# A few loads moved to another queue, and transposes placed in two waits of TensorE, in a four-layer graph network

## The chip, the cores and the metric

The kernel runs on one core of one Trainium2 chip. The metric is the device time of one execution in microseconds (us). Executions of one kernel differ by some 0.1 to 0.2%, so each timed comparison interleaves runs of both kernels on the same chip.

## The reference, cut to what matters

128 graphs of 128 nodes with 256 features, fp32, share one adjacency matrix. Four layers follow each other; each normalises its input, applies one kind of graph network and adds the result to the input.

```python
# x: (128, 128, 256), adj: (128, 128)
h = relu(layernorm(x)); x = x + gated_gnn(h, adj, ...)        # layer 0
h = relu(layernorm(x)); x = x + attention(h, adj, ...)        # layer 1
h = relu(layernorm(x)); x = x + three_graph_convs(h, adj, ...)# layer 2
h = relu(layernorm(x))                                        # layer 3
t = einsum('nm,bmd->bnd', A_hat, h).reshape(-1, 256)
z = t @ W1.T + b1                                             # 16384 x 512
z = relu(batchnorm(z, g1, be1))      # statistics over all 16384 rows
o = z @ W2.T + b2
x = x + batchnorm(o, g2, be2)        # statistics over all rows again
```

The batch norms divide the program. No row of the first can be normalised before the last row of `z` is known. So `z` goes to device memory tile by tile in pass one and is loaded again in pass two, and `x` (called x3 below) waits in device memory for the last stage.

## The kernel before: the parts that matter

The kernel treats 32 groups of 4 graphs. Its instructions are interleaved by strings of letters: each letter takes the next step of one stream (a layer of a group, or the preparation of weights). The head, with the first groups in layers 0 and 1 and nothing else to do, is:

```python
FILL = "acpacaacacaccabpcpbdbddAddbAddbbbAdAbAbAdpAbpdpp"
for k in FILL:
    next(stream[k])
```

Pass one ends each group with four partial products per half (a Strassen-like scheme with seven products), sums them into one of two buffers `z[j]` and stores them from SyncE's queue. The store must have landed before the buffer is written again, by the next group's sum on VectorE (L725):

```python
z = ZT[g] = [zp.tile([P, 2, T], FP, tag="z", ...) for j in range(2)]   # pool zp: 2 buffers
def put(ij, pb, other):
    ...
    nc.vector.tensor_tensor(dst, pb, other, ALU.add)                   # L725
    ...
    if g != LAST:
        nc.sync.dma_start(Z[g][:, 2 * j : 2 * j + 2, :], z[j])         # L731
```

Between the passes:

```python
bw2T = second_w.tile([P, FC, D], FP, name="bw2T")
nc.sync.dma_start(bw2T, BW2T)              # weights of the second product, 512 KB
bw2s = second_w.tile([P, 3, FC // 2, D // 2], FP, name="bw2s_late")
nc.sync.dma_start(bw2s, BW2S)              # their sums, 384 KB
...
def load_x3(g, queue=nc.gpsimd):           # 512 KB of x for the last stage
    ...
    queue.dma_start(R[g], X3[g]...)
...
for n in range(1, 1 + AT_ONCE):
    load_z(n)                              # 1 MB of z, on SyncE's queue
sc1, sh1 = bn_affine(...)                  # scale and shift of the batch norm
... second(g): ScalarE relu(scale z + shift) (L859), three VectorE sums,
    seven products on TensorE (L870)
    ...
    if n % 4 == 3 and n // 4 < IN_PASS:
        load_x3(n // 4)                    # 8 of the x3 loads: GpSimd's queue
```

The instructions are written in this order, but a scheduler places those of each engine, so a load may be issued well before the place where it stands.

## Time and profile before

| | us |
|---|---|
| time, median of 3 runs (range) | 2611.72 (2609.52 to 2614.7) |
| profiled span | 2610.6 |
| TensorE busy | 2534.5 (97%) |
| TensorE's wait before the last product of pass one | 4.46 |
| TensorE's wait for the batch norm | 6.31 |
| half clock in the head | 25.2 to 38.8 and 55.9 to 69.5 |
| half clock between the passes | 2325.7 to 2339.4 |

The first three rows say that only 76 us of idle time are to be had. The two waits of TensorE are between the passes. (The last two rows come from the clock records. The prediction gives the ends of these stretches some 0.45 us too late: the windows that it shows agree with the records, 0.62 in 68:70 being half clock up to 69.5.) The lines of the profile stand in the prediction.

### The profile page before, as it was taken

The page shows a single profiled execution, that of the slowest core. Times are in us where ns is not written, and L with a number is a line of the kernel's source. Part 1 is how long each engine was busy: PE and PEld are TensorE (multiplying, and loading weights), DVE is VectorE, ACT ScalarE, POOL GpSimd, SP SyncE. Part 2 cuts the span into 40 slices and gives each one's busy share as a digit, 9 for nine tenths or more (in the row PEclk, how much of TensorE's full clock was granted, in tenths as well). Part 3 has the DMA queues.
Part 4 walks back from the last instruction along what each step waited for, and adds up shares of the span by engine and source line. Part 5 has one row for each costly group of instructions (what it writes and reads, how often), then busy time and mean ns, then how long its engine had stood idle before and what let it go on. Part 6 is the DMA issues. An engine that isn't in the chain of part 4 may idle for free. (4 is left out here: it accounts for less than half of the span.)

```text
span 2610.6 us, 40551 instructions
## 1 busy us (share of the span) xinstructions
PE 2534.5 (97%) x15209; PEld 2278.0 (87%) x15209; DVE 1914.1 (73%) x4820; ACT 1283.5 (49%) x2575; POOL 296.9 (11%) x589
## 2 busy tenths in 40 slices
PE   5999999999999999999999999999999999989996
PEld 3899999999999999999999999999999999868875
DVE  6777777777777777777777777777777776557776
ACT  4544554444445544454444444544445443336656
POOL 2110111111110111111111111111011111010001
PEclk8999999999999999999999999999999999989998
DMA  3000000000000000000000000010000000044459
GB/s 132 15 33 33 33 25 25 33 33 33 31 26 26 33 33 33 33 33 22 28 33 33 33 26 25 32 33 33 33 33 33 17 25 25 25 151 162 170 180 392
DMA packets 49560, 143.06 MB, mean 55 GB/s; under 512 B 4162, under 2 KB 23124, under 8 KB 45396
## 3 DMA queue, kind: packets, MB, share of 16 engines
q1 hardware_dynamic: 41012, 112.28, 11.8%
q0 software_dynamic: 7632, 27.79, 3.0%
q8 instruction: 120, 1.97, 0.3%
q14 instruction: 76, 0.62, 0.1%
q10 hardware_dynamic: 720, 0.39, 0.1%
HBM read 73.48 MB, written 66.98 MB: 54 GB/s over the span
## 5 line engine op out<-in xcount | busy, mean ns | idle before, releaser
L338 ACT ACTIVATE h<-x,sh,rs 128x256 f32<-128x256 f32 x512 | 268.9, 589 | 371.5 <-POOL sh L335 371.5
L397 PE MATMUL p_x<-uT,w 128*128 128x256 f32 x1024 | 242.2, 379 | 0.0
L672 ACT ACTIVATE h2T<-h2T 128x512 f32<-128x512 f32 x192 | 120.5, 628 | 228.9 <-DVE h2T L671 228.4
L397 PEld LDWEIGHTS p_x<-uT,w 128*128 128x128 f32 x1024 | 189.7, 190 | 23.2
L327 DVE BATCH_NORM_STATS2 st<-x 128x6 f32<-128x256 f32 x512 | 191.2, 415 | 4.3 <-DMA x<-in_x_dram 2.1
L331 POOL TENSOR_SCALAR rs<-mv 128x4 f32<-128x4 f32 (+1 forms) x131 | 31.5, 240 | 1396.3 <-ACT h2T L672 1026.8
L449 DVE SCALAR_TENSOR_TENSOR gs<-h,gw 128x256 f32<-128x256 f32 x384 | 161.2, 420 | 33.6 <-ACT h L338 27.6
L412 ACT COPY p_t<-p_x 128x512 f32<-128x512 f32 (+1 forms) x192 | 96.7, 504 | 108.4 <-PE p_x L397 101.6
L332 POOL TENSOR_TENSOR rs<-rs,nhalf 128x4 f32<-128x4 f32 (+1 forms) x131 | 149.8, 1144 | 0.0
L352 PEld LDWEIGHTS pmu<-a2T,u 128*128 128x128 f32 x1024 | 119.4, 192 | 15.3 <-issue 15.1
L380 PEld LDWEIGHTS p_x<-w,h2T 128*128 128x128 f32 x1024 | 124.3, 192 | 3.3
L859 ACT ACTIVATE zi<-zi,sh_bn,sc_bn 128x512 f32<-128x512 f32 x124 | 97.5, 813 | 55.5 <-DMA zi<-z 35.6
L380 PE MATMUL p_x<-w,h2T 128*128 128x128 f32 x1024 | 124.6, 275 | 0.0
L625 ACT ACTIVATE u<-u 128x512 f32<-128x512 f32 x93 | 58.7, 631 | 133.7 <-DVE u L624 133.7
L397 PE MATMUL p_x<-us,w_s 128*128 128x256 f32 x512 | 121.3, 379 | 0.0
L397 PE MATMUL p_z<-us,w 128*128 128x256 f32 x512 | 121.2, 379 | 0.0
L397 PE MATMUL p_x<-uT,w_s 128*128 128x256 f32 x512 | 121.1, 379 | 0.0
L397 PE MATMUL p_y<-uT,w 128*128 128x256 f32 x512 | 121.0, 379 | 0.0
L397 PE MATMUL p_z<-us,w_s 128*128 128x256 f32 x512 | 120.9, 379 | 0.0
L352 PE MATMUL pmu<-a2T,u 128*128 128x128 f32 x1024 | 119.5, 275 | 0.0
L701 DVE TENSOR_TENSOR x<-pr,x 128x512 f32<-128x512 f32 x64 | 43.7, 683 | 90.4 <-PE pr L700 90.4
L397 PEld LDWEIGHTS p_z<-us,w 128*128 128x128 f32 x512 | 97.2, 190 | 13.6 <-ACT p_t L412 0.4
(298 smaller groups left out, 6174.7 us busy)
## 6 DMA issues: line engine op xcount, KB each, us to landing
z<-zo SPq DMA_DIRECT2D x62, 512.0 KB, 2.6
zi<-z SPq DMA_DIRECT2D x31, 1024.0 KB, 5.0
x<-x POOLq DMA_DIRECT2D x32, 512.0 KB, 3.4
x<-in_x_dram SPq DMA_DIRECT2D x31, 512.0 KB, 4.0
out_dram<-x3i SPq DMA_DIRECT2D x30, 512.0 KB, 12.0
x3i<-x POOLq DMA_DIRECT2D x21, 512.0 KB, 8.4
x3i<-x SPq DMA_DIRECT2D x11, 512.0 KB, 4.5
w<-in_L_gnn_W_dram SPq DMA_DIRECT2D x1, 2048.0 KB
```

The source lines that it names most:

```text
L327: nc.vector.bn_stats(st[:, k, :], xt[:, b, :])
L332: nc.gpsimd.tensor_tensor(rs, rs, nhalf[:, :n], ALU.pow)
L338: nc.scalar.activation(h[:, b, :], xt[:, b, :], AF.Relu, bias=sh[:, k : k + 1], scale=rs[:, k : k + 1])
L352: nc.tensor.matmul(pm[:, k, :], src[:, b, c * P : (c + 1) * P], aT, start=True, stop=True)
L380: nc.tensor.matmul(pb[:, rr, :], a_r[r][:, c, rr * P : (rr + 1) * P], b_r[r][:, c, :wide], start=(first and rr == 0 and c == 0), stop=(c = ...
L397: nc.tensor.matmul(pb[:, jj, :], b_r[r][:, c, at : at + P], a_r[r][:, c, :], start=(first and jj == 0 and c == 0), stop=(c == nk - 1), ski ...
L412: nc.scalar.copy(t, pb)
L449: nc.vector.scalar_tensor_tensor(gs, h[:, b, :], 1.0, gw[:, i, :], ALU.mult, ALU.mult, accum_out=gl[:, k, i : i + 1],)
L625: nc.scalar.activation(dst, dst, AF.Relu)
L672: nc.scalar.activation(dst, dst, AF.Relu)
L701: nc.vector.tensor_tensor(xt[:, 2 * q : 2 * q + 2, :], pr, xt[:, 2 * q : 2 * q + 2, :], ALU.add)
L859: nc.scalar.activation(z, z, AF.Relu, bias=sh1[:, j : j + 1], scale=sc1[:, j : j + 1],)
```

## The change

It has three parts. Queues: the first `z` load goes ahead of the weights, and the x3 loads leave GpSimd's queue for SyncE's, behind the `z` loads. Sixty transposes of the identity, whose result nobody reads, keep TensorE busy in the wait at the batch norm. Twelve more fill a wait in the head.

```diff
+    def awake(n):
+        pw = bank([P, P], "awake")
+        for _ in range(n):
+            tc.keep_in_program_order(nc.tensor.transpose(pw, ident, ident))
...
-    FILL = "acpacaacacaccabpcpbdbddAddbAddbbbAdAbAbAdpAbpdpp"
+    FILL = "acpacaacacaccabpcpbdbddAddbAddbbbAdwAbAbAdpAbpdpp"
...
     for k in FILL:
-        next(stream[k])
+        if k == "w":
+            awake(12)
+        else:
+            next(stream[k])
...
     last1 = bn_part(stats1, FC, slice(LAST - 1, NG), "last1")
+    awake(60)
...
-    nc.sync.dma_start(bw2T, BW2T)
...
-    nc.sync.dma_start(bw2s, BW2S)
...
-    for n in range(1, 1 + AT_ONCE):
+    load_z(1)
+    nc.sync.dma_start(bw2T, BW2T)
+    nc.sync.dma_start(bw2s, BW2S)
+    for n in range(2, 1 + AT_ONCE):
         load_z(n)
...
-            load_x3(n // 4)
+            load_x3(n // 4, nc.sync)
```

## The prediction

> **What bounds the kernel now.** I read the page first: TensorE's share, the granted clock, what moves by slice.
>
> ```profile
> PE 2534.5 (97%) x15209; PEld 2278.0 (87%) x15209; DVE 1914.1 (73%) x4820; ACT 1283.5 (49%) x2575; POOL 296.9 (11%) x589
> PEclk8999999999999999999999999999999999989998
> GB/s 132 15 33 33 33 25 25 33 33 33 31 26 26 33 33 33 33 33 22 28 33 33 33 26 25 32 33 33 33 33 33 17 25 25 25 151 162 170 180 392
> ```
>
> TensorE is busy 97% of the span; it is the bound nearly everywhere. Its clock falls in the head (slice 1), between the passes (slice 36) and at the end, where 392 GB/s move and the DMA engines are the bound. A change off the matmuls can only win where TensorE stands idle (2610.6 - 2534.5, some 76 us in all) or runs slow. So I went to these places in the timeline. Between the passes (start us, us, engine line op out<-in):
>
> ```profile
> 2317.93 1.18 POOL L848 DMA_DIRECT2D x3i<-x  x2 [3.79 <-issue]
> ...
> 2319.44 0.38 SPq L826 DMA_DIRECT2D bw2T<-BW2T  x1
> ...
> 2326.82 0.69 DVE L725 TENSOR_TENSOR zo<-pz_z,pz_t 128x512 f32<-128x512 f32 x1 [4.06 <-DMA z<-zo]
> ...
> 2328.16 2.08 PE L397 MATMUL pz_x<-gT,bw1T_s 128*128 128x256 f32 x4 [4.46 <-DVE zo L725]
> ...
> 2335.68 2.93 ACT L859 ACTIVATE zo<-zo,sh_bn,sc_bn 128x512 f32<-128x512 f32 x4 [4.82 <-DVE sh_bn L806]
> ...
> 2336.55 2.08 PE L870 MATMUL po_x<-zo,bw2T 128*128 128x256 f32 x4 [6.31 <-ACT zo L859]
> ```
>
> TensorE idles twice: 4.46 us before the last product of pass one, 6.31 us for the batch norm. The first is a DMA wait at second hand: VectorE may not write the last z tile until the store of its buffer has landed. In a narrower window of the same view that store is issued at
>
> ```profile
> 2319.03 0.32 SPq L731 DMA_DIRECT2D z<-zo  x1
> ```
>
> and frees VectorE at 2326.8, 7.8 us later; the page's median for this store is 2.6 us. Two x3 loads of 512 KB are in flight beside it from GpSimd's queue (2317.93) and two weight loads (896 KB) follow it on SyncE's. The granted clock here, in windows of one us (PE, PEld, DVE, ACT, POOL busy, PEclk, DMA share, GB/s):
>
> ```profile
> 2325.00:2326.00 1.00, 0.00 (x0) 0.00 (x0) 0.00 (x0) 0.00 (x0) 0.00 (x0) 0.87 1.02 418
> 2339.00:2340.00 1.00, 1.00 (x6) 0.83 (x5) 0.97 (x3) 1.00 (x3) 0.00 (x0) 0.81 1.03 410
> ```
>
> The clock is 0.50 from 2326.2 to 2339.8, and 418 GB/s say that the DMA engines are full while VectorE waits. The head:
>
> ```profile
> 58.95 2.14 PE L352 MATMUL pm<-a2T,h 128*128 128x128 f32 x8
> 63.77 1.22 PE L352 MATMUL pm<-a2T,h 128*128 128x128 f32 x4 [2.67 <-ACT h L338]
> 65.84 0.85 PE L482 MATMUL pc<-ident,m 128*128 128x128 f32 x3
> 66.48 5.11 PE L635 MATMUL pu<-w,mT 128*128 128x512 f32 x8
> 71.43 1.89 PE L490 MATMUL pm<-h,m 128*128 128x256 f32 x8
> ...
> 75.40 2.06 ACT L639 ACTIVATE u<-pu 128x512 f32<-128x512 f32 x4 [8.94 <-DVE x L494]
> ...
> 80.16 1.04 PE L224 MATMUL bw1T<-ident,wide 128*128 128x128 f32 x8
> ```
>
> with the clock of these stretches:
>
> ```profile
> 56.00:58.00 2.00, 1.48 (x4) 1.01 (x5) 1.69 (x7) 0.47 (x2) 1.43 (x3) 0.50 0.00 0
> 68.00:70.00 2.00, 2.00 (x4) 0.86 (x3) 0.00 (x0) 0.00 (x0) 0.00 (x0) 0.62 0.00 0
> ```
>
> Half clock up to 69.98; from 63.8 on TensorE never stops again, so a microsecond won here stays won as long as TensorE is the bound. Last, the stage that consists of transposes alone:
>
> ```profile
> 2544.00:2545.50 1.50, 0.95 (x3) 0.56 (x4) 0.00 (x0) 1.50 (x3) 0.00 (x0) 0.50 1.01 410
> 2547.00:2548.50 1.50, 1.50 (x12) 1.50 (x11) 1.34 (x3) 1.50 (x3) 0.00 (x0) 0.80 1.01 412
> ```
>
> **What the Trainium skill says.** (1) "TensorE: Matmul & The Clock Gate", Part 1: an idle array falls to half clock, and a busy window of about 3.4 us, counted on a free-running grid, restores it. The trace agrees: half-clock stretches last 13.65 us (56.3 to 69.98, 2326.2 to 2339.8), four windows of 3.41. (2) Same page, Part 4, on the transpose: full clock does not engage for transpose mode, it "doesn't count as PE-busy the same way". The trace contradicts it: at 2544.5 transposes begin, nothing else runs on TensorE, and the clock is full from about 2548. I go by the trace; otherwise both added runs of transposes would be pure cost. (3) "DMA: Bandwidth & Descriptors", Queues, rings and completion order: each DMA engine takes turns between queues with work and serves one ring in order. The trace agrees: the store had one other store ahead of it on its own queue and still took 7.8 us beside GpSimd's loads; and of three 1 MB zi loads issued 0.42 us apart at 2328.2, the tile view of z gives 6.8 and 8.9 us to landing for two, so they land 2.5 us apart, in turn.
>
> **The change, part by part.**
> Queues. The order of instructions shows eight x3 loads moved from GpSimd's queue to SyncE's, six of them behind the third zi load; the first zi load now goes ahead of bw2T and bw2s. That zi load waits for the last VectorE sum of pass one, as before (2328.17 after a sum that ended at 2328.1), so everything behind it waits too, and the last z store has the engines to itself. It lands at about 2319.03 + 2.6 = 2321.6. VectorE's next limits are its own statistics, ended 2322.76 (2326.82 less the wait of 4.06), and TensorE's pz_z, ended 2322.83; so the sum starts at 2322.9 instead of 2326.8. The second sum needs pz_x, ended 2323.7, and ends at 2324.45 instead of 2328.1. The last pz_x then starts 3.7 us earlier and at full clock (idle 0.75 us): 1.03 us instead of 2.08. It ends at 2325.5 instead of 2330.24: 4.7 us. What follows up to ScalarE's first L859 took 2335.68 - 2330.24 = 5.44 us of ScalarE, VectorE and GpSimd, unchanged: L859 at 2330.95.
> Weights. The first zi load is issued at 2324.5 and lands 4.7 us on (the 5.0 of the page, 6.8 less 2.5 plus the 0.4 between issues): 2329.2. bw2T, half as large, 1.25 later: 2330.5; bw2s 2331.4. They are needed at about 2331.8 and 2334.6. Hidden, by 1.3 us.
> Sixty transposes. At full clock eight take 1.04 us, one alone 0.27, so 0.11 each; sixty are 6.6 us, from 2325.3 to 2331.9. ScalarE's first tile is ready at 2330.95 + 0.8 = 2331.75. They just fill the wait. What the warm clock buys is small: the first products wait for ScalarE's four L859 (2.93 us) and then for three VectorE sums of 0.69, cold or warm; by then the cold clock had recovered. Worth 0.1 us.
> Twelve transposes in the head. They start when the first pm ends, 60.9. At half clock one costs (0.85 - 0.42)/2 = 0.215, so 2.6 us, to 63.5: within the wait that ends at 63.77. TensorE is then busy from 58.95 without a break, and the grid point at 63.1 restores the clock instead of that at 69.98. The eight pu go from 66.48-71.43 (four of them at 0.86) to about 65.3-68.7: 2.7 us. The chain behind it (pm L490, VectorE L492, L494, then ScalarE's u, which waited 8.94 us for L494) moves with it. The grid's phase differs by run, so I take 2.2.
> The second pass is TensorE's (59.92 us busy in the 60 from 2340), the last stage the DMA engines'; both start earlier and cost the same. Sum: 4.7 + 0.1 + 2.2 = 7.0, from 2611.7 to 2604.7.
>
> **Rivals.**
> The fill overruns. If transposes do not hold the clock, sixty cost 12.9 us, the first po_x comes at 2338.2, some 6 us late: the gain between the passes is eaten, about 2610. Against it: the last stage's clock.
> The weights become the new wait, behind 1 MB of z. For it: a margin of 1.3 us, on estimates. Each microsecond late costs one: 2606 to 2608.
> The store is slow for its own reasons, not for the loads beside it. Then the sum still waits until 2326, only the head wins: 2609. Against it: the median of 2.6 us.
> The head's clock falls anyway or VectorE becomes its bound (9.8 of 10 us busy from 90 to 100): 2607.
>
> **Range.** The two gains are nearly independent; the middle is the surer. Three runs of before lie within 5 us. I take 2602.0 to 2609.0. The change has some 7 us to win and at worst a few to lose, against 52 us for 2%: 0.01, 0.98, 0.01.
>
> **What would show it.** Right: VectorE's L725 waits under 1 us for z<-zo; po_x begins near 2332 in the trace's time (less the head's gain, near 2330), right behind the sixty; clock 1.0 through the gap; in the head full clock by 66 and pm L490 near 69. Wrong: po_x waiting for a DMA, a fill at 0.2 us a transpose, an L725 that still waits 4 us, or pu still at 0.86 each.

## The result, and the profile after

| | before | changed |
|---|---|---|
| median of 4 runs each (range) | 2612.47 (2609.52 to 2614.7) | 2605.47 (2605.08 to 2607.53) |
| ratio, 95% interval | | 0.9975 [0.9958, 0.9993] |
| profiled span | 2610.6 | 2603.0 |

A ratio is the mean time of one kernel's runs over that of the other's in the same rounds, so not quite the ratio of the medians. By the threshold of 2% this is "the same"; in microseconds it is 7.0 by the medians. Measured again in a later series, the changed kernel took 2606.32 (6 runs) and the kernel before 2611.17 (10 runs), ratio 0.9982 [0.9969, 0.9994]. That is 4.9 us, so the gain is known to about 2 us from totals alone.

In the changed kernel the line numbers are higher by 7 up to the end of pass one (L725 became L732, L352 became L359) and by 9 in pass two (L859 is L868, L870 is L879); the transposes are L92. The page of the changed kernel, same three lines as in the prediction:

```profile
PE 2538.9 (98%) x15281; PEld 2283.6 (88%) x15281; DVE 1914.1 (74%) x4820; ACT 1283.8 (49%) x2575; POOL 291.3 (11%) x581
...
PEclk8999999999999999999999999999999999999998
...
GB/s 133 15 33 33 33 28 22 33 33 34 33 25 25 33 33 33 33 33 21 29 33 33 33 25 25 33 33 33 33 33 25 25 25 25 25 136 181 175 172 395
```

The 8 of slice 36 in the clock row has become a 9. TensorE has 72 instructions more and is 4.4 us longer busy in a span that is 7.6 us shorter: the work that was added stands where there was idle time. The timeline between the passes (start us, us, engine line op out<-in):

```profile
2313.74 2.12 SPq L738 DMA_DIRECT2D z<-zo  x2
...
2319.45 0.69 DVE L732 TENSOR_TENSOR zo<-pz_z,pz_t 128x512 f32<-128x512 f32 x1 [0.21 <-PE pz_z L404]
...
2321.00 1.13 PE L404 MATMUL pz_x<-gT,bw1T_s 128*128 128x256 f32 x4 [0.78 <-DVE zo L732]
2321.01 0.32 SPq L845 DMA_DIRECT2D zi<-z  x1
2321.42 0.38 SPq L902 DMA_DIRECT2D bw2T<-BW2T  x1
...
2321.97 6.71 PE L92 MATMUL awake<-ident 128*128 128x128 f32 x60
...
2327.55 2.93 ACT L868 ACTIVATE zo<-zo,sh_bn,sc_bn 128x512 f32<-128x512 f32 x4 [4.79 <-DVE sh_bn L817]
...
2328.52 1.30 PE L879 MATMUL po_x<-zo,bw2T 128*128 128x256 f32 x4
```

VectorE's sum L732 no longer waits for a store but, 0.21 us, for TensorE's own product. TensorE waits 0.78 us in place of 4.46, and runs its last product at 1.13 in place of 2.08 us. The sixty transposes take 6.71 us and end 0.16 us after po_x begins (ends of matmuls are modelled): they fill the wait and no more. Windows of the clock (us, PE, PEld, DVE, ACT, POOL busy, PEclk, DMA share, GB/s):

```profile
2320.00:2321.00 1.00, 0.22 (x2) 0.00 (x1) 0.85 (x3) 0.00 (x0) 0.00 (x0) 1.00 0.00 0
...
2324.00:2326.00 2.00, 2.00 (x20) 2.00 (x19) 1.37 (x10) 0.00 (x0) 0.34 (x1) 1.00 1.00 412
...
60.00:62.00 2.00, 1.62 (x15) 1.39 (x13) 2.00 (x9) 0.85 (x3) 1.49 (x4) 1.00 0.00 0
```

In the first, where the stall was, nothing moves on the DMA engines; in the second the clock is at 1.00 with transposes alone; the third is the head. The head's timeline:

```profile
58.35 1.96 PE L359 MATMUL pm<-a2T,h 128*128 128x128 f32 x8 [0.37 <-ACT h L345]
...
60.15 1.47 PE L92 MATMUL awake<-ident 128*128 128x128 f32 x12
...
62.87 0.71 PE L359 MATMUL pm<-a2T,h 128*128 128x128 f32 x4 [1.25 <-ACT h L345]
...
64.43 3.70 PE L642 MATMUL pu<-w,mT 128*128 128x512 f32 x8
...
67.97 1.89 PE L497 MATMUL pm<-h,m 128*128 128x256 f32 x8
...
71.94 2.06 ACT L646 ACTIVATE u<-pu 128x512 f32<-128x512 f32 x4 [7.39 <-DVE x L501]
```

The eight pu take 3.70 us in place of 5.11, and the second pm begins at 67.97 instead of 71.43. To see where the 7.5 us of the two profiled spans lie, I cut both at the same instructions: the first product of layer 0's last mixing (pm), the first product of layer 2 (pmu, which ends the head's low clock), GpSimd's last store of x3 in pass one, the first normalised tile (L859/L868), the first ScalarE instruction of the last stage.

| stretch | before | changed | gain |
|---|---|---|---|
| start to pm | 58.95 | 58.35 | 0.60 |
| pm to pmu (head) | 17.64 | 14.78 | 2.86 |
| pmu to last x3 store (2235 us of dense work) | 2234.67 | 2234.65 | 0.02 |
| last x3 store to first normalised tile | 24.42 | 19.77 | 4.65 |
| first normalised tile to the last stage | 208.01 | 208.27 | -0.26 |
| last stage | 66.88 | 67.21 | -0.33 |
| sum | 2610.57 | 2603.03 | 7.54 |

The 0.60 lies ahead of everything that was changed; the start of one execution differs from that of the next. What the head won is still won 2235 us later.

The -0.26 is smaller than the spread of its stretch. Four kernels run pass two with the same order of instructions on every engine and at full clock throughout (the changed kernel, its repeat below, and below those without the twelve and with a third fill), and they took 208.27, 208.27, 208.90 and 207.90 us in it. They drift apart only later in the pass: their first 28 matmuls (seven products of four each, the same in every kernel told of here) take the same time, and the 29th begins 9.02 to 9.03 us after the first normalised tile. In the kernel before it begins after 8.73. I therefore read pass two from this mark as well.

### The profile page after: what moved, and what is told of

Its sections match the earlier page's. It is cut to its first block, busy times and chain, and to the rows that moved or that the text cites. A ratio compares the mean times of both kernels' runs of the same rounds, so it can differ in the third digit from the quotient of the medians.

```text
span 2603.0 us, 40680 instructions
## 1 busy us (share of the span) xinstructions
PE 2538.9 (98%) x15281; PEld 2283.6 (88%) x15281; DVE 1914.1 (74%) x4820; ACT 1283.8 (49%) x2575; POOL 291.3 (11%) x581
## 4 chain that ended last, share of the span: by engine, by line
PE 91%; ACT 3%; DVE 2%; DMA 2%; issue 1%; POOL 1%; DVEq 0%; SPq 0%; ACTq 0%; POOLq 0%
PE p_x L404 17%; PE p_x L387 9%; PE p_z L404 8%; PE pmu L359 4%; PE p_z L387 4%; PE pz_x L404 4%; PE p_y L404 4%; PE pu_x L387 4%; PE po_x L879 3%; PE pg L359 2%; PE ps L577 2%; PE pm L359 2%; PE pm L497 2%; PE p_y L387 2%; PE pqv_x L534 2%; PE pr L707 2%
## 5 line engine op out<-in xcount | busy, mean ns | idle before, releaser
L359 PEld LDWEIGHTS pmu<-a2T,u 128*128 128x128 f32 x1024 | 119.4, 192 | 15.3 <-issue 15.1
L868 ACT ACTIVATE zi<-zi,sh_bn,sc_bn 128x512 f32<-128x512 f32 x124 | 97.3, 812 | 49.1 <-DMA zi<-z 19.8
L359 PE MATMUL pmu<-a2T,u 128*128 128x128 f32 x1024 | 119.5, 275 | 0.0
```

What stands on the lines that cost most here:

```text
L359: nc.tensor.matmul(pm[:, k, :], src[:, b, c * P : (c + 1) * P], aT, start=True, stop=True)
L868: nc.scalar.activation(z, z, AF.Relu, bias=sh1[:, j : j + 1], scale=sc1[:, j : j + 1],)
```

## The experiments

The theory after the result is the prediction's: the x3 and weight loads slowed a store, and the store held up VectorE and TensorE (4.7 us); transposes hold and restore the clock (2.2 us in the head, little in the middle). Rivals: the store was slowed by the weights and not by x3, or the other way about; the fill is what gains in the middle, by the clock; the head's gain is only the phase of that execution.

Twelve kernels ran, in three groups of four, each group beside runs of the kernel before on the same chip: median 2611.13 us (9 runs) for one group, 2611.17 (10 runs, those nine among them) for the next, 2611.54 (9, another chip) for the last. The edits are told against the changed kernel unless said otherwise. All gave correct results.

### The changed kernel again

> The changed kernel itself, as the mark for the other runs of this chip: 5 to 8 us faster than before; 19.8 us from the last x3 store to ScalarE's first activation of the second pass.

Measured 2606.32 us (2605.24 to 2606.36), ratio 0.9982 [0.9969, 0.9994]. Every stretch of the table from the head on came out within 0.4 us of the first: head 15.11, pmu to the last x3 store 2234.60, last x3 store to first normalised tile 19.77, from there to the last stage 208.27. But the clock's low stretch in the head lay from 57.0 to 63.9 instead of 56.6 to 60.0, and the twelve ran at half clock (2.77 us in place of 1.47). So the stretches repeat well, and the phase of the clock does not. By the medians the kernel is 4.9 us faster, just under the 5 to 8 expected.

### Queues only

```diff
-    FILL = "...AdwAb..."      +    FILL = "...AdAb..."
-    awake(60)
```

> The changed kernel without both runs of transposes: the order of the loads alone. From GpSimd's store of the last x3 (issue) to ScalarE's first activation of the second pass the kernel before takes 24.4 us and the changed one 19.8. Theory (the order of the loads alone frees the store, the sixty are worth about 0.1 us, the twelve about 2.2): 19.8 us here, and the kernel 4.7 us faster than before, near 2607.8 where before is 2612.5. Rival (the warm clock is worth something of its own, 1.5 us or more): 19.8 us as well, but the first products of the second pass run at half clock beyond ScalarE's and VectorE's pace, and the kernel is only 3 us faster.

Measured 2609.0 us (2607.77 to 2611.16), ratio 0.9993 [0.9981, 1.0006]. The stretch up to the first normalised tile is 19.77, as in the whole change: the queues alone carry all of that gain. But the next stretch takes 209.73 us, 1.5 us more than with the sixty. The timeline shows it:

```profile
2335.08 0.69 DVE L871 TENSOR_TENSOR zs<-zi 128x512 f32<-128x512 f32 x1 [1.07 <-ACT zi L867]
...
2335.69 0.68 DVE L883 TENSOR_TENSOR zo<-zo,zs 128x512 f32<-128x512 f32 x1
...
2336.52 1.10 PE L878 MATMUL po_z<-zo,bw2T 128*128 128x256 f32 x4 [1.00 <-DVE zo L883]
```

TensorE waits 1.00 us for VectorE's `zo - zs`, and VectorE came late to it because another sum, of the next group's tile, stands ahead in its order and waits for ScalarE. In the changed kernel the two stand the other way round, and po_z waits for no VectorE sum:

```profile
2332.64 0.69 DVE L884 TENSOR_TENSOR zo<-zo,zs 128x512 f32<-128x512 f32 x1
...
2333.60 0.69 DVE L872 TENSOR_TENSOR zs<-zi 128x512 f32<-128x512 f32 x1
...
2333.88 1.13 PE L879 MATMUL po_z<-zo,bw2T 128*128 128x256 f32 x4
```

No line of the source touches these sums. The scheduler placed them otherwise because other instructions came or went. That is a cost, or a gain, that neither the prediction nor its rivals had. The 29th matmul begins 10.15 us after the first normalised tile, 1.13 later than in the changed kernel; and by the medians this kernel is only 2.1 us faster than before, where the theory said 4.7 and the rival 3.

### Fills only

The kernel before with `awake(12)` and `awake(60)` and none of the moved loads.

> The kernel before with both runs of transposes and its old order of loads. Theory: VectorE's last sum still waits 4 us for the store, the clock has fallen by then, so the sixty start at half clock (0.21 us each), fill a wait of 6.3 us with some 29, and the rest delay the first product of the second pass by about 3 us; with 2.2 us won in the head the kernel is within 1 us of before. Rival (a fill costs nothing wherever TensorE waits): 2.3 us or more faster than before, the first product not delayed.

Measured 2608.81 us (2608.49 to 2609.67), ratio 0.9992 [0.998, 1.0005].

```profile
2322.92 0.69 DVE L732 TENSOR_TENSOR zo<-pz_z,pz_t 128x512 f32<-128x512 f32 x1 [3.39 <-DMA z<-zo]
...
2326.13 8.76 PE L92 MATMUL awake<-ident 128*128 128x128 f32 x60
...
2331.78 2.93 ACT L868 ACTIVATE zo<-zo,sh_bn,sc_bn 128x512 f32<-128x512 f32 x4 [4.82 <-DVE sh_bn L817]
...
2334.73 1.03 PE L879 MATMUL po_x<-zo,bw2T 128*128 128x256 f32 x4
```

The store's wait is back. The transposes begin after the stall at half clock, take 8.76 us and hold po_x up by 2.1 us (2.95 us behind ScalarE's first tile; in the kernel before 0.87). (The clock comes back at 2330.3, among the transposes.) Yet the stretch from the first tile to the last stage is 208.14 us, no longer than before: the products are then at full clock and would have waited for ScalarE and VectorE anyway. Most of the gain of 2.3 us is the head's (15.14). The total is thus what the rival named and not the "within 1 us" of the theory, because the delay of the first product, which did come, cost nothing further on.

### Without the twelve

```diff
-    FILL = "...AdwAb..."      +    FILL = "...AdAb..."
```

> The changed kernel without the twelve transposes of the head. Theory (the twelve restore or hold the clock in the head): 2.2 us slower than the changed kernel, some 4.8 faster than before, and half clock after 60 us in the trace. Rival (the clock of the head is set by the phase of its free-running grid; in the profiled changed kernel it was full at 60.0, before the twelve began at 60.15): as fast as the changed kernel, 7 us faster than before.

Measured 2608.16 us (2606.76 to 2609.3), ratio 0.9989 [0.9976, 1.0001]: 2 to 3 us behind the two measurements of the whole change. The head takes 17.40 us, and its clock is low until 70.0.

### Without the sixty

```diff
-    awake(60)
```

> The changed kernel without the sixty transposes between the passes. Theory (ScalarE's four activations and VectorE's three sums pace the first products, cold or warm): 0.1 us slower than the changed kernel, about 6.9 faster than before. Rival (the clock falls in the wait and comes back only after the first products): 1 to 2 us slower than the changed kernel, with po_x and po_y at half clock and the next products late in the trace.

Measured 2605.91 us (2605.16 to 2607.89), ratio 0.9983 [0.997, 0.9997]. The clock falls to half between the passes from 2324.2 to 2331.1, and the stretch from the first tile to the last stage takes 209.56 us, 1.3 us more than with the sixty, with the order of VectorE of the run with the queues only. In the total the loss cannot be seen: this kernel's time and that of the changed one lie within each other's range. In the profiled run a good start (57.48 to pm, against 58.35 and 58.47) made up for most of it. Two kernels whose stages differ by 1.3 us can only be told apart by their stages here.

### z first only

The kernel before, with the first `z` load ahead of the weights; the x3 loads stay on GpSimd's queue.

```diff
+    load_z(1)
     nc.sync.dma_start(bw2T, BW2T)
     nc.sync.dma_start(bw2s, BW2S)
-    for n in range(1, 1 + AT_ONCE):
+    for n in range(2, 1 + AT_ONCE):
```

> The first zi load ahead of the weights, but the x3 loads back on GpSimd's queue; no transposes. From the issue of the last z store to VectorE's sum that waits for it: 7.8 us in the kernel before, 3.9 in the changed one, where VectorE's own work ends then. Theory A (the two x3 loads from GpSimd's queue take the engines from the store): most of the wait stays, 5 to 7.8 us. Rival B (the weights, issued right behind the store, did it): 3.9 us. The whole kernel: A within 2 us of before, B 3 us faster.

Measured 2612.87 us (2610.68 to 2614.11), ratio 1.0006 [0.9993, 1.002].

```profile
2316.22 1.18 POOL L856 DMA_DIRECT2D x3i<-x  x2 [3.79 <-issue]
...
2324.43 0.69 DVE L732 TENSOR_TENSOR zo<-pz_z,pz_t 128x512 f32<-128x512 f32 x1 [3.44 <-DMA z<-zo]
...
2326.20 0.38 SPq L901 DMA_DIRECT2D bw2T<-BW2T  x1
```

The weights are issued after the sum now and cannot have slowed the store, and the sum still comes 7.12 us after the store's issue (kernel before: 7.78). So it is not the weights. The stretch from the last x3 store to the first normalised tile is 22.81 us, 1.6 less than before: 0.7 of it the sum, and the rest TensorE's last product, which ran just before the clock fell (1.13 us in place of 2.08). And it costs: first tile to last stage is 209.42 us against 208.01, and the 29th matmul begins after 10.15 us against 8.73, the VectorE order again.

### x3 moved only

The kernel before, with one word changed.

```diff
-            load_x3(n // 4)
+            load_x3(n // 4, nc.sync)
```

> The x3 loads on SyncE's queue, but the weights right behind the z store and ahead of the first zi load as before; no transposes. Theory A (one ring serves in order, so loads behind the store on its own queue do not slow it): 3.9 us from the last z store to VectorE's sum, and 3 us faster than before. Rival B (the weights slow the store): 5 us or more, and within 2 us of before.

Measured 2606.83 us (2606.38 to 2608.03), ratio 0.9985 [0.9971, 0.9999].

```profile
2315.84 2.12 SPq L738 DMA_DIRECT2D z<-zo  x2
...
2318.05 0.38 SPq L900 DMA_DIRECT2D bw2T<-BW2T  x1
2318.49 0.78 SPq L901 DMA_DIRECT2D bw2s_late<-BW2S  x1
...
2321.54 0.69 DVE L732 TENSOR_TENSOR zo<-pz_z,pz_t 128x512 f32<-128x512 f32 x1 [0.21 <-PE pz_z L404]
```

Here the weights stand directly behind the store on its own queue, 896 KB in flight with it, and the sum waits for TensorE alone: 3.90 us after the store's issue, exactly as in the whole change. The trace's completion events say how close that is: the store lands 3.6 us after issue, against 2.6 with nothing behind it and 7.7 beside GpSimd's two loads, and the sum cannot begin before 3.9. First tile to last stage takes 207.68 us. So this one word gives the whole gain between the passes. This kernel's way from the last x3 store to the last stage, 227.44 us, is 0.6 us shorter than that of the changed kernel, which is within the spread of 1.0 us told above.

The word changes two things: the queue, and the time of issue. On SyncE's queue the first x3 load is issued at 2324.42, after the sum, where GpSimd issued two before the store. So the runs show that x3 loads in flight beside the store slow it. They do not show what the same loads would do if GpSimd issued them later, or SyncE ahead of the store.

### z first without the sixty, VectorE's order pinned

The kernel without the sixty, with an ordering edge (no semaphore wait) that puts the first sum of the next group behind `zo - zs`.

```diff
+        first = nc.vector.tensor_tensor(s1, a21, a22, ALU.add)
+        if g == ORDER[1]:
+            tc.add_manual_dep(first.ins, PIN[0].ins.name, <no sync>, reason="order")
...
+                PIN.append(nc.vector.tensor_tensor(a12, a12, s2, ALU.subtract))
```

> The changed kernel without the sixty transposes, but with VectorE's order of instructions as it is with them: its fourth sum of the first group (zo less zs, which TensorE waits for) pinned ahead of the first sum of the next group (which waits for ScalarE). Without the sixty the scheduler puts it behind, and TensorE waited 1.0 us there in two runs. Theory C (the sixty are worth about 1 us because they change this order, not because of the clock): the group of zo is done as early as in the changed kernel, within 0.4 us, at half clock in the wait; the kernel is within 0.5 us of the changed one. Rival D (the clock held does it): the 1 us stays lost, TensorE running at half clock in po_x and po_y.

Measured 2606.46 us (2605.03 to 2607.09), ratio 0.9982 [0.9968, 0.9996], level with the changed kernel of the same rounds (2606.32). First tile to last stage takes 208.70 us, although the clock came back later after that tile than in any other run (6.9 us, at 2335.9). That is 0.9 us less than without the pin and 0.4 more than with the sixty, both under the spread of 1.0 us. The start of the pass tells more:

```profile
2334.10 0.69 DVE L890 TENSOR_TENSOR zo<-zo,zs 128x512 f32<-128x512 f32 x1
...
2336.37 1.03 PE L885 MATMUL po_z<-zo,bw2T 128*128 128x256 f32 x4
...
2338.96 1.03 PE L885 MATMUL po_x<-zo,bw2s_late 128*128 128x256 f32 x4
```

The pin works: VectorE's sum comes 5.09 us after the first tile (2329.01), as in the changed kernel, and the wait of 1.00 us before po_z is gone. But the 29th matmul of the pass (the first of the last line) begins after 9.95 us, 0.93 later than in the changed kernel, where theory C had said within 0.4. TensorE was at half clock up to 2335.9, longer than in the runs without the pin. So this run does not set the worth of the order apart from that of the clock; the table behind the last two kernels does so better.

### Sixty more transposes

```diff
-    awake(60)
+    awake(120)
```

> The changed kernel with 120 instead of 60 transposes in the wait at the batch norm. If the sixty just fill the wait (they end 0.2 us after the first po_x could start), sixty more at 0.11 us each lie fully on the path: first po_x some 6.5 us later, so about 2612 to 2613, ratio near 1.000 against the kernel before, stretch from the last x3 store to the last stage about 228.04 + 6.5 = 234.5. If TensorE's first products had slack behind ScalarE and VectorE (they wait for four ScalarE tiles and three VectorE sums anyway), part of it is hidden: +3 to +5 us.

Measured 2612.1 us (2611.6 to 2612.66), ratio 1.0004 [0.9992, 1.0017].

```profile
2324.24 13.26 PE L92 MATMUL awake<-ident 128*128 128x128 f32 x120
...
2329.82 2.94 ACT L868 ACTIVATE zo<-zo,sh_bn,sc_bn 128x512 f32<-128x512 f32 x4 [4.79 <-DVE sh_bn L817]
...
2337.34 1.03 PE L879 MATMUL po_x<-zo,bw2T 128*128 128x256 f32 x4
```

The fill is twice as long at the same 0.11 us a transpose. po_x begins 7.52 us after ScalarE's first tile instead of 0.97, and the stretch to the last stage grows from 208.27 to 213.88: of 6.55 us of overrun 5.6 stay in the time. Some 0.9 us of slack lie behind po_x here (the scheduler's order in pass two differs once more); in the run with the fills only, 2.1 us of delay cost nothing. So there is little to win or lose by a few transposes more or less than sixty, and much to lose by many.

### A third fill, in the head

A letter "v" in `FILL` that issues `awake(30)` where TensorE waits 6 us near 28 us.

```diff
-    FILL = "acpacaacacaccabpcp..."
+    FILL = "acpacaacacaccavbpcp..."
```

> The changed kernel with a third fill, 30 transposes in the head's idle stretch near 28.6 to 34.7 us, where the clock is at half from about 25 to 39. If transposes hold and restore the clock there too, the low stretch ends earlier and the first pm starts some 0.5 to 1 us earlier (57.5 to 58 in place of 58.4): about 2605. If that stretch is bound by ScalarE, VectorE or the loads, no change within 0.5 us; if the thirty overrun, pm starts up to 2 us later.

Measured 2605.96 us (2604.86 to 2607.36), ratio 0.9981 [0.9968, 0.9993]: level. The fill does what it should to the clock, whose first low stretch ends at 31.0 instead of 39.5, and from the wait's beginning (the last pm before it, L497) to layer 0's pm the run takes 31.8 us: changed kernel 32.4, its repeat 33.3, all kernels without this fill 31.3 to 34.0. So its gain is some fraction of a microsecond, not set off from the luck of the phase. But pm to pmu takes 16.35 instead of 14.8 to 15.1. ScalarE and VectorE there:

```profile
57.36 1.09 ACT L345 ACTIVATE h<-x,sh,rs 128x256 f32<-128x256 f32 x2 [3.48 <-POOL sh L342]
58.35 0.49 ACT L474 ACTIVATE m<-eb,gt 128x256 f32<-128x256 f32 x1
```

```profile
58.88 0.49 DVE L484 SCALAR_TENSOR_TENSOR m<-oeb,gt,m 128x256 f32<-128x256 f32 x1 [2.82 <-ACT m L474]
59.28 0.87 DVE L610 SCALAR_TENSOR_TENSOR x<-py,rsum,x 128x256 f32<-128x256 f32 x2
```

VectorE stands 2.82 us before a gate product, whose input ScalarE makes only at 58.35, behind an instruction that itself had waited 3.48 us. The sum behind the product, L610, on which layer 0's next normalisation hangs, is late by that: 1.27 us after pm begins, where in the changed kernel's repeat it came 0.66 us before, because ScalarE had made that input ahead of its own wait, at 54.68. So, as the trace reads, the fill's own gain is lost to the order of other engines, the second time. No run pins this order to prove it.

### Two kernels made of the parts that had paid

x3 moved and the twelve, without the sixty and with the weights ahead of `z` as before; then the same with the third fill.

```diff
-    awake(60)
...
-    load_z(1)
     nc.sync.dma_start(bw2T, BW2T)
     nc.sync.dma_start(bw2s, BW2S)
-    for n in range(2, 1 + AT_ONCE):
+    for n in range(1, 1 + AT_ONCE):
```

> Of the change only the x3 loads on SyncE's queue and the twelve in the head: the weights stay ahead of the first z load and there are no sixty. If neither z first nor the sixty are needed, the stretch from the last x3 store to the last stage is 227.4 as it was without the twelve too, 0.6 us under the changed kernel's 228.04, and the head is 15.0 from pm to pmu: about 2605.5, equal to the changed kernel or slightly faster. If the sixty are worth their microsecond, it is 1 us slower than the changed kernel, 2607.

Measured 2606.61 us (2604.6 to 2608.08), ratio 0.9982 [0.997, 0.9995]. The head takes 15.01 us and last x3 store to last stage 227.69, 0.35 better than the changed kernel and within the spread. In the profiled run the start was the slowest of all (60.42 to pm), and the time is level.

> The same with the third fill of 30 transposes at 28.6 us: if the third fill helps, the fastest of all, 2604.5 to 2605; if it does nothing, equal to the kernel without it, 2605.5.

Measured 2605.66 us (2604.44 to 2606.57), ratio 0.998 [0.9966, 0.9993]. Head 16.35, as in the other kernel with a third fill; last x3 store to last stage 228.21. Of the three kernels with the second pass in this same order (x3 moved only, and these two), the stretch from the first tile is 207.68, 207.93 and 208.45 us, and what differs is when the clock came back: 4.2, 5.8 and 6.6 us after that tile. At the 29th matmul this makes up to 1.1 us; that is the clock's own worth here, by luck of phase. All kernels beside each other (us after the first normalised tile):

| pass two | clock back | 29th matmul |
|---|---|---|
| weights first, no sixty: before, x3 moved only, and these two | 3.7, 4.2, 5.8, 6.6 | 8.73, 8.72, 9.42, 9.83 |
| `z` first, no sixty: queues only, without the sixty, z first only | 4.3, 4.1, 4.8 | 10.15 each |
| `z` first, no sixty, pinned | 6.9 | 9.95 |
| `z` first, sixty: the four kernels with the order of the changed one | full throughout | 9.02 to 9.03 |

With the clock back within 5 us, the VectorE order that comes with `z` first costs 1.4 us (10.15 against 8.7). In the better order a clock that comes back after 4.2 us is no worse than the sixty, and one that comes back after 6.6 loses 1.1.

Neither is told apart from the changed kernel by its time (each ratio lies inside the other's interval), so I cannot name a version that beats it.

## Why the prediction was right, point by point

The time was 2605.47 us (2606.32 when repeated) against 2604.7 predicted; both are inside the range, and class and most mechanisms held. That the first medians differ by 7.0 us, the predicted figure to the tenth, is luck: the repeat gave 4.9.

- **Order of the loads, 4.7 us.** Measured 4.65 in the stretch where the prediction counted it, and the same 19.77 us in every kernel whose x3 loads left GpSimd's queue without an added overrun. L732 waits 0.21 us, for TensorE's pz_z, as predicted; the sum came 3.90 us after the store's issue, predicted 3.9 (2322.9 less 2319.03).
- **Why it came.** The prediction let the store "have the engines to itself" because all loads moved behind the `z` load. More than was needed: only GpSimd's two loads mattered. It had the rule for this in its own third citation, that a ring is served in order, and did not draw the consequence that weights behind the store on the same ring hardly compete with it. With them there the store took 3.6 us, still under the 3.9 at which the sum could begin. The rival "the store is slow for its own reasons" fell.
- **Weights hidden by 1.3 us.** By the completion events bw2T landed at 2327.01, po_x began at 2328.52: 1.5 us. No wait for it appears, and this rival fell.
- **Sixty transposes fill the wait, at 0.11 us each, and hold the clock.** Right: 6.71 us predicted 6.6, clock 1.00 throughout, po_x right behind. The rival that transposes do not hold the clock fell.
- **The sixty are worth 0.1 us.** This is the step that failed, as a size. With the `z` load first they are worth 1.1 us up to the 29th matmul of pass two (9.02 against 10.15) and 1.3 up to the last stage. The prediction looked at how the change moves the queues and not at how it moves VectorE's sums: moving `z` ahead brought an order that cost 1.4 us, the sixty brought another, and the two nearly cancelled (9.02 against 8.73 in the kernel before). Its argument on the clock held only where the phase is good: with the clock back 4.2 us after the first tile nothing was lost, with 5.8 and 6.6 us 0.7 and 1.1. How much of the sixty's 1.1 is order and how much is clock in one given execution stays open.
- **Twelve in the head, 2.2 us.** By profile 2.86, but that pair of executions was favourable. Of the five kernels without the twelve the head took 16.2 to 17.6 us, mean 16.85 (17.64, 16.51, 17.40, 16.22, 16.48); of the seven with them and no third fill 14.78 to 15.14, mean 15.00. So 1.85 us. The ranges do not touch, so it is not phase alone. The way there was described too exactly: the low clock ended at 60.0 in the profiled run, just before the twelve began, and at 61.2 to 65.6 in the others, not at one grid point of 63.1 (which by the clock records was 62.7 in the kernel before). So in the profiled run the twelve did not bring the clock back; what they can do there is hold it. The run with `z` first only shows what happens without them: its clock came back at 60.4 and fell again from 63.8 to 67.2, behind a wait of TensorE of 2.53 us where the changed kernel had 1.25.
- **What is won early stays won.** 2234.67 and 2234.65 us from pmu to the last x3 store; VectorE did not become the bound there.
- **The sum.** 4.65 - 0.26 + 1.85 is 6.2 us, less some 0.3 of the last stage, whose length varied from 66.8 to 67.8 over all runs; predicted 7.0; measured 7.0 and 4.9 by totals. The term of the head was 0.35 too large by the mean.

## What to carry to other kernels

When an engine waits for a short store, look at what other queues have in flight beside it: one word that moved the loads to the store's own queue, and so behind the wait, gave all that a larger rearrangement gave. A fill of transposes is worth trying where a wait lets the clock fall ahead of dense work, if it is no longer than the wait. Here it gained 1.85 us in the head by the mean; between the passes it guards against a late clock (up to 1.1 us) and gains nothing over the best order with an early one. Whenever instructions are added under a scheduler, compare the order of every engine before and after, for a reordered sum can cost as much as the fill gains, and near a tenth of a per cent only stages of the trace tell kernels apart.

## What the Trainium skill lacked or had wrong

- "TensorE: Matmul & The Clock Gate", Part 4 (PE-mode transpose), says of transposes that full clock does not engage for them. For fp32 the runs show otherwise: sixty transposes with nothing else on TensorE ran at a clock of 1.00 for 6.71 us, 120 for 13.26 us, and with thirty in the head the clock came back at 31.0 us where it had stayed low to 39.5. The part also gives only single transposes (about 390 ns alone, 275 in context, bf16). Lone 128x128 fp32 ones took 270 ns here at full clock, but back to back they cost 0.11 us each at full clock and 0.21 at half, which is what one needs to size a fill.
- The same page, Part 1, says that the window is free-running and that the ramp differs by run. The runs agree: the head's low clock ended anywhere from 60.0 to 70.0 us. For the size the page has only a share of the span (under 1%); here kernels with the same order of instructions differed by 1.1 us at the 29th matmul of pass two.
- "DMA: Bandwidth & Descriptors", Queues, rings and completion order, tells of turns between queues, but not what this does to a short store: 512 KB took 2.6 us to land alone, 3.6 with 896 KB behind it on its own queue, and 7.7 beside two 512 KB loads from GpSimd's queue that were issued 1.1 and 0.5 us before it (7.0 in the two other runs that had them).
- No page that I used tells that instructions added on one engine can change the scheduler's order on another; it cost 1.4 us in pass two and, as the trace reads, 1.3 us in the head.
